# Sixteen half products ahead of the scan's first chunk in place of thirteen, and one function table loaded ahead of softplus

## The chip, the cores and the metric

The kernel runs on one core of one Trainium2 chip. The metric is the time of the program on the device in microseconds (us), the median of several runs; lower is better. The core has five engines that run at the same time and wait for each other by semaphores: TensorE (PE, matrix products; its weight loads are told apart as PEld), VectorE (DVE), ScalarE (ACT, activation functions and copies), GpSimd (POOL) and SyncE (SP, which issues most of the transfers between DRAM and the on-chip memory).

## The reference, cut to what matters

A network of four layers works on an image x of 1024 channels by 64 x 64 pixels in fp32. Each layer adds its output to x, and takes x normalized over groups of 32 channels.

- Layer 0 is a scan over the channels, layers 1 and 3 are pointwise products with a 1024 x 1024 matrix and a bias.
- Layer 2 is a selective scan. Its input is multiplied by a 3072 x 1024 matrix and passed through silu, which gives three parts of 1024 channels: `x_ssm`, `res` and `gate`. `x_ssm` goes through a convolution of width 3 along the pixels and silu, and from it 34 numbers per pixel are made: for each of two heads a step `dt = softplus(...)`, eight values B and eight values C. For each head the pixels are put in an order of its own, and a state of 512 x 8 numbers runs over the 4096 pixels: `h = exp(dt * A) * h + dt * B * x`, `y = C . h + D * x`. Then `y` goes back into image order, and the layer's output is `silu(W_out (y * silu(gate) + res))`.

Softplus is computed as `max(v, 0) + log(1 + exp(-|v|))`, with a correction of the rounding.

## The kernel before, in words

**The products.** A product with a 1024 x 1024 matrix is done by Strassen's scheme (in Winograd's form) on halves: 7 products of half matrices in place of 8. The pixels are in 8 blocks of 512, taken as 4 pairs; a pair gives the two columns of the scheme. `run` goes over the pairs, and `multiply` goes for each pair over two groups `g` of output channels, with 7 products each in the order `b21, b11, b22, t2, t3, t1, t4`. Each product takes one tile of weights (`weights`, L827, issued by SP, five tiles in turn) and one set of right sides (`B`), and adds into two PSUM banks, one for each of two blocks `o` of 128 output channels. `multiply` hands over control after the first block and after the second. What lies between two such points is a *half product*, or unit: 4 matrix products of 128 x 128 by 128 x 512. In the profile each fp32 product is two records of line L844, so a unit is 8 records. When a product is complete, its results are taken: `put` makes a copy (ScalarE), `add` adds to it (VectorE).

**Layer 2 in stages.** First the matrix of `x_ssm` (`WX`) is run over all pairs, with the convolution (L1068, L1071), the turn into pixel rows (L1090, L1092) and the 34 numbers following behind. `finish(pair)` takes the 34 numbers of a pair of blocks, makes softplus of `dt` and writes rows into a table `tok_d` in DRAM, one for each head and pixel. Its steps on ScalarE are Abs (L1194), Exp (L1195) and Ln (L1205), and between and around them stand VectorE's splits of numbers into a coarse and a fine part (L1188, L1190), the steps of the correction (L1200 to L1208) and the transfers to `tok_d` (L1225, L1227), by SP and for the last pair's second head by GpSimd. `finish` runs for each of the four pairs; the first three lie within the products of `WX`, and the last one stands between the last units there and the scan.

Then comes the scan, 74 chunks of 56 pixels of each head. For chunk k, GpSimd gathers its rows from `tok_d` by an indirect transfer (L1321), all of the last `finish` being in the table first; ScalarE makes `ds` (L1329), TensorE makes sums and turns (`turn_rows`, L1335 and L1336), VectorE spreads the decays (`spread_decay`, L1342 to L1350), ScalarE takes Exp (L1418), TensorE crosses B with C (`cross`, L1357), VectorE weighs (`weigh`, L1365 to L1370, into `G`), TensorE applies (`apply`, L1374, `py`), ScalarE hands 8 rows of state for each head to the next chunk (L1377) and copies the result (L1379), and GpSimd scatters it to DRAM (L1383). The steps of the loop are pipelined: step k turns chunk k+1, weighs and applies chunk k-1 and crosses chunk k.

**What fills the scan.** The matrix of `res` (`WR`) doesn't depend on the scan. Its 112 units are handed out by `next_units(upto)`, one at a call as long as fewer than `upto` are given. Eight are given while the last convolutions run, the others up to `first` ahead of chunk 0, and the rest are spread evenly over the loop's 76 steps, at most two in a step:

```python
total, first, given = NP * 2 * NG * 7, 13, 0
...
for k in range(5):
    gather(k)
while given < first:
    next_units(total)
    if len(silus) > 3:
        activate(4)
step_sums(0)
for k in range(-1, NK + 1):
    upto = first + (k + 2) * (total - first) // (NK + 2)
```

For `WR`, `put` is `put2b` (L1030, a ScalarE copy into a tile `rg`), `add` is `add2b` (L1034, a VectorE add), and of finished tiles four at a time are passed through silu by `activate` (L1040) and stored by SP (L1042). During the scan GpSimd also makes sums of weights for layer 3 (`sum_weights2`, L468 to L500, `s` in the profile).

After the scan layer 2's gate and output products and layer 3 follow as one long stage in two levels of the scheme (`two_steps`, L1727).

**The order of the work.** The engines PE, DVE, ACT and POOL are in `tc.manual_schedule` throughout layer 2, so that they take instructions about in the order in which the program writes them; SP is not. ScalarE holds one set of function tables at a time; where the next function needs another set, an instruction ACT_TABLE_LOAD stands ahead of it, put there by the compiler. `nc.scalar.preload_act_table_set(name)` writes such a load into the program by hand, with the set of that name.

Of the kernel before, what the change touches and what calls it, by code (L numbers as in the profile page):

```python
# [50 lines left out]
NG = KH // OG  # L51
NP = NB // 2
# [42 lines left out]
def tile_net(ctx: ExitStack, tc: tile.TileContext, x, par_d, cst_d, w_d, w2_d, dbcw_d, out):  # L95
    nc = tc.nc
# [4 lines left out]
    def ps_tp(name):  # L101
        return psum.tile([P, FB], F32, tag="tp", name=name)
# [798 lines left out]
    def run(pairs, mats, make, put, add, before=None, after=None, last_eng=None, fine=False, tell=False, B=None, begun=None, quick=False):  # L901

        def sets(i):
            B = begun if begun and i == 0 else {"name": f"{mats[0]}_{pairs[i]}"}

            def steps():
                if before is not None:  # L910
                    before(pairs[i])
                yield from b_sets(B, lambda t, ct, col: make(t, ct, 2 * pairs[i] + col), quick=quick or i == 0,
                                  eng=last_eng if i == len(pairs) - 1 else None)
            return B, steps()


        if B is None:
            B, steps = sets(0)
            for _ in range(5 if begun is None else 0):
                next(steps)  # L920
        else:
            steps = iter(())
        for i, pair in enumerate(pairs):
            late = steps
            nxt, steps = sets(i + 1) if i + 1 < len(pairs) else (None, iter(()))
            left = 7 * NG * len(mats)
            for m in mats:
                for half in multiply(m, B, lambda o, c, ps: put(m, o, 2 * pair + c, ps),
                                     lambda o, c, ps: add(m, o, 2 * pair + c, ps), fine, begun and i == 0):
                    if half:  # L930
                        yield True
                        if half == "rest":
                            for _ in range(5):
                                next(late)
                        continue
                    if tell:
                        yield False
                    left -= 1
                    next(steps if left < 5 else late, None)
                    yield  # L940
            if after is not None:
                after(pair)
            last_B[0], B = B, nxt

    def normed(norm):
        def make(t, ct, nb):
            scale, bias = norm[ct]
            nc.scalar.activation(t, X[nb][:, ct, :], AF.Identity, bias=bias, scale=scale)  # L948
        return make
# [95 lines left out]
    with tc.tile_pool(name="l2a", bufs=2) as pa, tc.tile_pool(name="l2a2", bufs=1) as pa2, \  # L1045
# [11 lines left out]
        def tok_rows(t0, q, n, c0, h):  # L1057
            return tok_d[h * N + t0 : h * N + t0 + q * P, c0 : c0 + n].rearrange("(q p) c -> p q c", p=P)
# [91 lines left out]
        def finish(pair):  # L1150
            n = 2 * TPB
            yield
            acc = accs[pair].rearrange("p b (h f) -> p b h f", h=HEADS)
            if pair == NP - 1:

                nc.vector.memset(acc[:, n], 0.0)
                nc.scalar.activation(end, end, AF.Silu)
                pe = ps_tp("end_pt")
                nc.tensor.transpose(pe[:CT, :P], end, ident)
                et = pa.tile([CT, P], F32, name="end_t", bufs=1)  # L1160
                nc.scalar.copy(et, pe[:CT, :P])
                for h in range(HEADS):
                    nc.sync.dma_start(tok_d[h * N + N - 1 : h * N + N, :DH].rearrange("a (b c) -> (a b) c", c=P),
                                      et[h * KH : (h + 1) * KH, :])
                pz = ps_tp("end_dbc")
                for o in range(CT):
                    nc.tensor.matmul(pz[:1, : HEADS * NF], end[:, o : o + 1], both[:, o, P:], start=(o == 0), stop=(o == CT - 1))
                nc.vector.tensor_tensor(accs[pair][:1, n], pz[:1, : HEADS * NF], dbcb[:1], ALU.add)
                n += 1


            def t(name):
                w = pa.tile([P, 2 * TPB + 1, HEADS], F32, tag=f"sp_{name}", name=f"sp_{name}{pair}", bufs=1)
                return w[:, :n]

            f = acc[:, :n]
            v, m, e, u, d = t("v"), t("m"), t("e"), t("u"), t("d")
            lots = [(0, TPB, row), (TPB, TPB, row)]
            if pair == NP - 1:
                lots = [(0, TPB, row), (TPB, 3, spare[0]), (TPB + 3, n - TPB - 3, spare[1])]  # L1180

            def split(b0, q, to, at, c):
                for h in range(HEADS):
                    x = f[:, b0 : b0 + q, h, c : c + S].unsqueeze(2).to_broadcast([P, q, 2, S])
                    parts = to[:, :q, h, at : at + KW].rearrange(
                        "p b (a c) -> p b a c", c=HS)[:, :, :, h * S : (h + 1) * S]
                    hi, lo = parts[:, :, HI[at]], parts[:, :, LO[at]]
                    nc.vector.tensor_scalar(hi.bitcast(I32), x.bitcast(I32), 12, 12, ALU.logical_shift_right,  # L1188
                                            ALU.logical_shift_left)
                    nc.vector.tensor_tensor(lo, x, hi, ALU.subtract)  # L1190

            nc.vector.tensor_copy(v, f[:, :, :, 0])
            nc.vector.tensor_scalar(m, v, 0.0, None, ALU.max)
            nc.scalar.activation(e, v, AF.Abs)  # L1194
            nc.scalar.activation(e, e, AF.Exp, scale=-1.0)  # L1195
            for i, lot in enumerate(lots):
                if i == 0 or lot[2] is not row:
                    split(*lot, CF, 1 + S)

            nc.vector.tensor_scalar(u, e, 1.0, None, ALU.add)  # L1200
            nc.vector.tensor_scalar(d, u, -1.0, None, ALU.add)
            nc.vector.tensor_tensor(d, e, d, ALU.subtract)
            nc.vector.reciprocal(v, u)
            nc.vector.tensor_tensor(d, d, v, ALU.mult)
            nc.scalar.activation(u, u, AF.Ln)  # L1205
            nc.vector.tensor_tensor(u, u, d, ALU.add)
            nc.vector.tensor_tensor(u, u, m, ALU.add)
            nc.vector.tensor_tensor(f[:, :, :, 1 : 1 + S], f[:, :, :, 1 : 1 + S],  # L1208
                                    u.unsqueeze(3).to_broadcast([P, n, HEADS, S]), ALU.mult)
            for i, (b0, q, to) in enumerate(lots):  # L1210
                if i and to is row:
                    yield
                    yield
                    split(b0, q, to, CF, 1 + S)
                split(b0, q, to, BF, 1)
                nc.vector.tensor_copy(to[:, :q, :, DT], u[:, b0 : b0 + q])
                t0 = pair * 2 * FB + b0 * P - 1
                full = min(q, 2 * TPB - b0)
                for h in range(HEADS):
                    dma = nc.gpsimd if h and pair == NP - 1 else nc.sync  # L1220
                    if t0 < 0:
                        dma.dma_start(tok_d[h * N : h * N + P - 1, DH:], to[1:, 0, h, :])
                        dma.dma_start(tok_rows(t0 + P, q - 1, NF2, DH, h), to[:, 1:q, h, :])
                    else:
                        dma.dma_start(tok_rows(t0, full, NF2, DH, h), to[:, :full, h, :])  # L1225
                    if full < q:
                        dma.dma_start(tok_d[h * N + N - 1 : h * N + N, DH:], to[:1, full, h, :])  # L1227

        forget(LATE)
        with tc.manual_schedule(engines={E_.DVE, E_.PE, E_.Pool, E_.Activation}):  # L1230
# [5 lines left out]
            for half in run(EARLY + LATE, [WX], normed(norm2), put2a, add2a, before2,  # L1236
# [26 lines left out]
                if i > 14 and i % 14 == 4:  # L1263
                    ends = finish(i // 14 - 1)
# [15 lines left out]

            forget(EARLY)
            units = run([3, 2] + EARLY, [WR], normed(norm2), put2b, add2b, before2, fine=True, B=last_B[0])
            total, first, given = NP * 2 * NG * 7, 13, 0

            def next_units(upto):
                nonlocal given
# [16 lines left out]
            for _ in finish(NP - 1):  # L1303
                pass
# [548 lines left out]
```

## Time and profile before

| what | us |
|---|---|
| median of 3 runs | 2696.77 (2696.16 to 2699.23) |
| the profiled execution, whole | 2699.02 |
| its span, first to last instruction | 2696.9 |
| TensorE busy | 2568.1 (95%) |
| VectorE busy | 1833.7 (68%) |
| ScalarE busy | 1084.6 (40%) |
| GpSimd busy | 1217.9 (45%) |
| matrix products of layers 1 and 2 up to the scan's end (L844) | 1200.6 |
| the scan, from chunk 0's first matrix product to the last unit | about 1149 to 1627 |

The profiled execution is 2.1 us longer than its span (what lies around it) and 2.25 us longer than the median. Times in the profile's views are counted from the start of the span. Busy times are totals over the whole; an engine that is 95% busy may still stand still where a stage begins, so the stage around the change has to be read by its own times. A matrix product's duration as listed overlaps the next one's: a record of L844 lasts 0.60 us but the next one starts 0.43 us later. In a timeline the number in brackets is the time that the engine stood idle ahead of the instruction, and behind the arrow stands what ended it.

### The profile page before, as it was taken

To read this page: it belongs to the slowest core of one execution; us is meant where nothing else is said; L and a number is where in the kernel's file an instruction comes from. 1 tells how busy PE (TensorE), PEld (TensorE's weight loads), DVE (VectorE), ACT (ScalarE), POOL (GpSimd) and SP (SyncE) were. 2 spreads that over 40 slices of the span, in tenths; PEclk is the share of its full clock that TensorE was granted. 3 is DMA by queue.
4 is the path that set the end of the run, shared out by engine and by line. 5 is a ranking of instruction groups with operands and counts; after the bars stand their busy time and mean duration, and the time that the engine had idled before them with its cause. 6 is when DMAs were issued, how large, how long until landed. Compare 5 with 4: busy or idle time off the path is not lost.

```text
span 2696.9 us, 30618 instructions
## 1 busy us (share of the span) xinstructions
PE 2568.1 (95%) x9520; PEld 1714.4 (64%) x9520; DVE 1833.7 (68%) x3870; ACT 1084.6 (40%) x1839; POOL 1217.9 (45%) x1100
## 2 busy tenths in 40 slices
PE   4788999999999999999999999999999999899998
PEld 3674444444555555444444447888888888788887
DVE  7996866655555654367787775577585676877877
ACT  3783110103656554465767664332243233311220
POOL 4154123232133243136474635575575565554544
PEclk9898999999999999999999999999999999999999
DMA  7245467547555577477667846889899798788896
GB/s 290 102 165 203 147 226 257 182 135 242 152 168 134 145 192 192 119 233 237 212 209 232 303 155 193 236 242 296 223 300 268 240 312 226 257 301 294 302 323 212
DMA packets 422741, 597.22 MB, mean 221 GB/s; under 512 B 141972, under 2 KB 210707, under 8 KB 419508
## 3 DMA queue, kind: packets, MB, share of 16 engines
q1 hardware_dynamic: 298020, 367.89, 42.7%
q10 hardware_dynamic: 91456, 136.33, 14.4%
q0 software_dynamic: 33104, 91.04, 13.3%
q8 instruction: 77, 1.26, 0.2%
q14 instruction: 84, 0.69, 0.1%
HBM read 435.10 MB, written 160.05 MB: 221 GB/s over the span
## 4 chain that ended last, share of the span: by engine, by line
PE 79%; DVE 10%; ACT 7%; DMA 2%; issue 1%; SPq 0%; POOL 0%; DVEq 0%; ACTq 0%; POOLq 0%
PE mm L844 36%; PE q_P6P L1727 5%; PE q_P5P L1727 5%; PE q_P7P L1727 5%; PE q_P2P L1727 5%; PE q_P4P L1727 5%; PE q_P3P L1727 5%; PE q_P1P L1727 5%; PE l2pt L1090 2%; PE py L1374 2%; DVE xt L632 1%; DVE cvp L1071 1%; DVE stats L554 1%; ACT b L948 1%; ACT xt L598 1%
## 5 line engine op out<-in xcount | busy, mean ns | idle before, releaser
L844 PE MATMUL mm<-t,w 128*128 128x512 f32 x1536 | 686.1, 598 | 0.0
L844 PE MATMUL mm<-b,w 128*128 128x512 f32 x1152 | 514.5, 598 | 4.0 <-ACT b L948 2.9
L844 PEld LDWEIGHTS mm<-t,w 128*128 128x128 f32 x1536 | 287.5, 191 | 323.6 <-issue 318.2
L844 PEld LDWEIGHTS mm<-b,w 128*128 128x128 f32 x1152 | 216.1, 191 | 252.6 <-issue 240.9
L1383 POOL DMA_INDIRECT y_rows<-g,dst x74 | 73.8, 997 | 198.2 <-ACT g L1379 166.6
L1071 DVE SCALAR_TENSOR_TENSOR cvp<-xs,par,cvp 128x512 f32<-128x512 f32 x128 | 95.4, 754 | 76.9 <-ACT cvp L1068 74.6
L1696 ACT COPY qQ<-q_P5P 128x512 f32<-128x512 f32 x48 | 28.1, 586 | 294.1 <-PE q_P5P L1727 278.3
L468 POOL TENSOR_TENSOR s<-s 128x256 f32<-128x256 f32 (+3 forms) x120 | 130.6, 1093 | 7.5
L1377 ACT COPY g<-py 8x512 f32<-8x512 f32 x146 | 83.9, 574 | 107.9 <-PE py L1374 106.9
L1122 DVE TENSOR_TENSOR xs<-mm,xs 128x512 f32<-128x512 f32 x64 | 41.8, 685 | 118.1 <-PE mm L844 118.1
L1098 POOL TENSOR_TENSOR acc<-l2xt,acc 128x136 f32<-128x136 f32 x56 | 29.2, 522 | 191.9 <-ACT l2xt L1092 191.0
L963 DVE SCALAR_TENSOR_TENSOR image<-mm,par,image 128x512 f32<-128x512 f32 x64 | 47.2, 747 | 95.3 <-PE mm L844 95.3
L1090 PEld LDWEIGHTS l2pt<-both,cv 128*128 128x128 f32 x512 | 76.2, 190 | 36.3 <-issue 22.5
L802 POOL TENSOR_TENSOR t<-t,b 128x512 f32<-128x512 f32 x40 | 55.7, 1420 | 93.8 <-DVE t L802 93.7
L948 ACT ACTIVATE b<-image,gnl_bias,gnl_r_r 128x512 f32<-128x512 f32 x48 | 36.9, 807 | 143.3 <-PE mm L844 130.6
L1495 ACT ACTIVATE qb<-x_x_b,gn_bias,gn_r_r 128x512 f32<-128x512 f32 x64 | 48.8, 807 | 112.2 <-DVE qQ L1657 36.0
L1727 PE MATMUL q_P4P<-t_t,wq_P4P 128*128 128x256 f32 x384 | 92.5, 384 | 1.4 <-DVE qV L1704 1.4
L1727 PE MATMUL q_P1P<-t_b,wq_P1P 128*128 128x256 f32 x384 | 91.7, 383 | 1.5 <-POOL t_b L1491 1.5
L1704 DVE TENSOR_TENSOR qV<-q_P4P,qV 128x512 f32<-128x512 f32 x96 | 64.9, 687 | 38.6 <-PE q_P4P L1727 37.0
L1491 POOL TENSOR_TENSOR t_t<-qt 128x512 f32<-128x512 f32 x23 | 29.6, 1288 | 136.3 <-DVE qt L1491 76.5
L1727 PE MATMUL q_P5P<-t_t,wq_P5P 128*128 128x256 f32 x384 | 90.8, 379 | 0.0
L1727 PE MATMUL q_P6P<-t_t,wq_P6P 128*128 128x256 f32 x384 | 90.7, 379 | 0.0
(419 smaller groups left out, 6004.7 us busy)
## 6 DMA issues: line engine op xcount, KB each, us to landing
w<-s_d SPq DMA_DIRECT2D x96, 512.0 KB, 4.8
w<-in_w_dram SPq DMA_DIRECT2D x72, 512.0 KB, 4.3
x_x_b<-x_d ACTq DMA_DIRECT2D x28, 1024.0 KB, 6.1
image<-x_d SPq DMA_DIRECT2D x12, 2048.0 KB, 10.9
wq_P6P<-s_d SPq DMA_DIRECT2D x84, 256.0 KB, 5.0
wq_P7P<-s_d SPq DMA_DIRECT2D x84, 256.0 KB, 6.1
wq_P5P<-s_d SPq DMA_DIRECT2D x84, 256.0 KB, 3.6
wq_P3P<-s_d SPq DMA_DIRECT2D x84, 256.0 KB, 3.7
```

Of the source, the lines that this page charges most:

```text
L468: eng.tensor_tensor(out, a, b, ALU.subtract)
L802: eng.tensor_tensor(B[name][k], B[one][k], B[two][k], ALU.subtract)
L844: nc.tensor.matmul(to[o], w[:, k, o * P : (o + 1) * P], B[name][k], start=(fresh and k == 0), stop=(k == KH - 1), skip_group_check=True)
L948: nc.scalar.activation(t, X[nb][:, ct, :], AF.Identity, bias=bias, scale=scale)
L1071: nc.vector.scalar_tensor_tensor(cv, xo[:, at + t : at + t + FB], pcol("dww", 3 * o + t), cv, ALU.mult, ALU.add)
L1090: nc.tensor.matmul(pt[:, q * NV : (q + 1) * NV], cv[:, (q0 + q) * P : (q0 + q + 1) * P], both[:, o, :], start=True, stop=True)
L1374: nc.tensor.matmul(py, G2[k % 2], rows[k][:, :DH], start=True, stop=True)
L1377: nc.scalar.copy(rows[k + 1][h * LC : h * LC + S, :DH], py[h * LC : h * LC + S])
L1383: nc.gpsimd.indirect_dma_start(out=y_views[k % len(y_views)][:, :], out_offset=bass.IndirectOffsetOnAxis(ap=dst_[:, k : k + 1], axis=0), i ...
L1495: nc.scalar.activation(tile_of(j, name)[:, k], held[j, "x", name][:, k], AF.Identity, bias=bias, scale=scale)
L1704: nc.vector.tensor_tensor(to, ps, to, ALU.add)
L1727: nc.tensor.matmul(ps[:, o, :], w[:, k, o * P : (o + 1) * P], rhs[:, k, :], start=(new and o == 0 and k == 0), stop=(k == 1), skip_group_c ...
```

## The change

Two lines. In `finish`, ahead of Abs, a load of the table set `natural_log_exp_and_others` is written into the program; it is not limited to the last pair, so it stands there four times. And 16 units in place of 13 are given ahead of the scan's chunk 0, so that 96 in place of 99 are spread over its 76 steps. The three are the second half of `t4` of the first group, and both halves of `b21` of the second group.

```diff
@@ -1191,6 +1191,7 @@
             nc.vector.tensor_copy(v, f[:, :, :, 0])
             nc.vector.tensor_scalar(m, v, 0.0, None, ALU.max)
+            nc.scalar.preload_act_table_set("natural_log_exp_and_others")
             nc.scalar.activation(e, v, AF.Abs)
             nc.scalar.activation(e, e, AF.Exp, scale=-1.0)
             for i, lot in enumerate(lots):
@@ -1280,7 +1281,7 @@
             forget(EARLY)
             units = run([3, 2] + EARLY, [WR], normed(norm2), put2b, add2b, before2, fine=True, B=last_B[0])
-            total, first, given = NP * 2 * NG * 7, 13, 0
+            total, first, given = NP * 2 * NG * 7, 16, 0
```

## The prediction

> **What bounds the kernel now.** I read the slices first (TensorE at 9 tenths nearly everywhere), then the chain of waits (79% TensorE), then the timelines of TensorE, ScalarE and VectorE where the scan begins. TensorE's timeline there, columns start, length, engine, line, work, and in brackets the idle time before it:
>
> ```profile
> 1124.63 14.86 PE L844 MATMUL mm<-t,w 128*128 128x512 f32 x34
> 1148.86 0.98 PE L1335 MATMUL pr<-cst,g 128*128 128x192 f32 x2 [9.38 <-ACT ds L1329]
> 1149.63 0.53 PE L1336 MATMUL pr<-ds,cst 128*128 128x64 f32 x2
> 1149.95 5.68 PE L844 MATMUL mm<-t,w 128*128 128x512 f32 x8
> 1155.48 0.49 PE L1335 MATMUL pr<-cst,g 128*128 128x192 f32 x2
> 1155.80 0.33 PE L1336 MATMUL pr<-ds,cst 128*128 128x64 f32 x2
> ```
>
> The reader sees the end of the 13 half products that `first` puts ahead of the scan (each is 8 records of L844), then 9.38 us of nothing, then chunk 0. The half product after the hole takes 5.68 us; later ones take 3.65. The stretches (length, busy of TensorE, weight loads, VectorE, ScalarE, GpSimd, granted clock, DMA share, GB/s) show why, and how full the scan is after it:
>
> ```profile
> 1139.00:1150.00 11.00, 1.62 (x7) 1.17 (x5) 0.00 (x0) 0.35 (x1) 7.86 (x13) 0.72 0.79 229
> 1150.00:1156.00 6.00, 6.00 (x14) 2.84 (x13) 3.08 (x8) 2.50 (x4) 0.52 (x1) 0.66 0.79 314
> 1160.00:1628.00 468.00, 456.91 (x1285) 227.53 (x1283) 356.47 (x796) 316.72 (x551) 244.82 (x242) 1.00 0.70 224
> ```
>
> The clock falls to about 0.7 through the hole and returns by 1156. From 1160 to 1628 us TensorE idles 11.1 us in 468: the scan's length is TensorE's work, 99 half products and the 74 chunks' own matmuls.
>
> What the hole waits for is a chain: softplus of the last pair, the split rows, their transfers to `tok_d` (landing 1139.7), gather 0 (issued 1141.88), `ds` of chunk 0 at 1148.51. Its first part, on ScalarE and then VectorE:
>
> ```profile
> 1125.65 0.22 ACT L1194 ACTIVATE sp_e<-sp_v 128x18 f32<-128x18 f32 x1 [1.25 <-DVE sp_v L1192]
> 1125.89 1.28 ACT L1195 ACT_TABLE_LOAD   x1
> 1127.18 0.22 ACT L1195 ACTIVATE sp_e<-sp_e 128x18 f32<-128x18 f32 x1
> 1127.31 0.57 ACT L1030 COPY rg<-mm 128x512 f32<-128x512 f32 x1
> 1127.89 1.28 ACT L1205 ACT_TABLE_LOAD   x1
> 1129.19 0.22 ACT L1205 ACTIVATE sp_u<-sp_u 128x18 f32<-128x18 f32 x1
> ```
> ```profile
> 1129.44 0.18 DVE L1206 TENSOR_TENSOR sp_u<-sp_u,sp_d 128x18 f32<-128x18 f32 x1 [0.66 <-ACT sp_u L1205]
> ```
>
> Two loads of 1.28 us, but VectorE, busy with the splits of L1188 and L1190 until 1127.8, loses only the 0.66 us ahead of L1206.
>
> **What the Trainium skill says.** "ScalarE: Activation LUTs", "Table sets: the hidden batching unit": one set, natural_log_exp_and_others, holds both exp and ln, and abs is in every set; so the added load should make those of Exp and Ln unnecessary. The trace agrees in kind: Abs and the copies bring no load here, and Exp and Ln each bring one, from different sets. Its section "What ACT_TABLE_LOAD costs" gives 1283 ns and 1380 ns of drain. The load agrees (1283 ns); the drain doesn't show, Exp follows 0.01 us after its load; I use 1.28. "TensorE: Matmul & The Clock Gate", "What's actually happening", says that the clock is halved after about 3.4 us of idling and needs as long a busy time to come back. The trace agrees: 9.38 us idle, then some 6 us at 0.66.
>
> **The change, part by part.**
>
> *Three half products moved.* 24 records of L844 that ran in the scan run ahead of chunk 0. In the chain of waits 8 records take 3.44 us, so 3 take 10.3 us. TensorE finished unit 13 at 1139.36 (34 records of 0.43 us from 1124.74); unit 16 should end at 1149.7, so the hole is filled and overrun by 0.8 us. Can they run there? Unit 14 is the rest of `t4`, 15 and 16 are `b21` of the second group. Their right sides are the B tiles just used. Loads run five products ahead on SP: the three weights from the input tensor at 1103.0, 1109.9 and 1120.7 are in order `t4`, `b21` and `b11`, ahead of the row transfers. Their PSUM bank is the one that `t1` leaves, and VectorE's last L1034 on it starts by 1138. So nothing should stop them.
>
> What else moves with them: two VectorE adds of `t4` (L1034, 0.68 us each) at about 1143, when VectorE is empty; and two ScalarE copies of `b21` (L1030, 0.59 us each), the second after unit 16's end. On ScalarE `ds` of chunk 0 may stand behind this copy. Then it runs at 1150.2 to 1150.6 and the second matmul pair of chunk 0 (L1336) waits for it; if it goes ahead, there is no wait. I price it 0 to 0.6 us. Their `rg` tiles come from memory of the earlier pools, free at 1139.7 when the row transfers land. On SP the weights of a later product, held at 1155.67 until unit 14 was done, go out near 1145, between the gathers: 0.5 MB at the 0.4 MB per us that the DMA slices show there at most is 1.3 us (estimate). Gather 0, at 1148.5 now, would come by 1149.1 at worst with the 0.66 us from below, and TensorE is busy until 1149.7. On GpSimd nothing moves.
>
> *The clock.* With no hole, chunk 0's four records take 0.50 us, in place of 1.29, and the unit after them 3.49, in place of 5.48 (all by the chain of waits): 2.8 us.
>
> Sum at the start of chunk 1's matmuls (1155.6 before): chunk 0 starts 0.8 us later (1149.7 for 1148.9), 2.8 us come back, 0 to 0.6 go to `ds`: 1.4 to 2.0 us earlier. From there the scan has 3 half products fewer: 10.3 us. Together 11.7 to 12.3.
>
> *Given back.* The scan has 76 steps; 23 hold two half products now, 20 after. A step of one half product takes 5.07 us. In the one at 1601 VectorE ends G at 1603.8 and `py` uses it at 1605.24: 1.4 us of slack. Where VectorE or ScalarE has a burst in such a step TensorE waits, as these rows (total, times, longest) of the waits from 1160 to 1628 us say:
>
> ```profile
> PE py L1374 <- DVE G L1370: 4.7, 4, 1.4
> PE pr L1336 <- ACT ds L1329: 3.5, 4, 0.9
> PE py L1374 <- ACT rg L1040: 1.5, 1, 1.5
> ```
>
> 9.7 us in 9 places. Three more short steps, and another alignment of all, may remove some or add some: I take 0.7 us more, with -3 and +6 as bounds.
>
> *The function table.* It is in `finish` for all four pairs: 4 loads in, 8 out, 5.1 us less of ScalarE. In the last pair it can run from 1124.4, when ScalarE is idle for 1.25 us, and end about when `sp_v` is there. Exp comes 1.2 us earlier but VectorE is not waiting for it; Ln comes earlier and saves the 0.66 us. In the new order gather 0 is no longer what TensorE waits for, so this is worth 0 on the path; it covers the DMA delay above. In the other three pairs TensorE is busy throughout but for 1.79 us at 909.6, where VectorE's sort is late; there VectorE may gain up to 0.55 us. I take 0.3, with 0 to 0.6. If the load, which depends on no data, slips ahead of a Silu, that pair pays two loads more, 2.6 us of ScalarE, still largely covered.
>
> **Sum:** 12.0 + 0.3 - 0.7 = 11.6; I take **11.3 us**, the low side of the `ds` wait. The profiled execution took 2699.02 us (span 2696.9), so it would give 2687.7; against the median of the runs, 2696.77, it is 2685.5.
>
> **Rivals.**
> - *Half of it given back* (the short steps become bound by the chain weigh, G, `py`). For it: only 1.4 us of slack. Against it: most short steps show no wait. Five more waits of 1.2 us: gain 5 to 7, 2690.5.
> - *No change.* Units 14 to 16 don't run in the hole (a bank, a weight, an order on an engine), or the scan is paced by its recurrence, so that its start sets its end. Against it: 97.6% busy, and weights there by 1121. Time 2695 to 2697.
> - *Slower.* The place is the one-unit step. If the shift of three units puts the bursts of VectorE (two adds 1.28 and a difference L802 1.20 in a row) into steps without a second unit all along, each costs up to 1.5 us. It decides when waits rise by more than 12 us, from 11 to 23; slower by over 0.2% takes 28 us, 19 steps at 1.5 us, in place of 9. Then 2703. Against it: the number of bursts per unit is fixed and the spread of steps nearly the same.
> - *It doesn't do what it says:* the preload leaves a load at Exp or Ln. Then the last part costs 0.66 us of the cover and no more than 1 us.
>
> **How the numbers follow.** 0.2% is 5.4 us, about what a measurement can tell from no change: faster means below 2691.4. Full gain 0.74, half 0.15 (two thirds of it below that line), no change 0.06, slower 0.05. So faster 0.84, same 0.11, slower 0.05. The range from 2682.0 takes 3 us of waits removed and some spread of runs; to 2692.0 it takes the case of half.
>
> **What would show it.** Right: no idle at TensorE between 1124 and 1149, the first L1335 near 1149.7 and within 0.6 us its L1336, then 3.5 us units at clock 1.00; 41 table loads in place of 45, none at Exp and Ln of `finish`; the last L844 near 1616. Wrong: a bracket of some us ahead of a unit or of the first L1336, or waits of `py` for G or for ScalarE above 15 us in the scan. The whole falls if the scan's end stays near 1627.

## The result, and the profile after

| | before | after |
|---|---|---|
| median of 6 runs each, us | 2697.82 (2695.36 to 2700.26) | 2684.88 (2680.42 to 2686.91) |
| ratio of the run times, 95% interval | | 0.9948 (0.9938 to 0.9959) |
| the profiled execution, whole, us | 2699.02 | 2685.99 |
| its span, us | 2696.9 | 2684.1 |
| table loads on ScalarE | 45 | 41 |

The kernel became faster by 12.9 us in the medians, or by 14.0 us by the ratio (0.52%; 11.1 to 16.7 by its interval). The profiles of both kernels are single executions. TensorE's timeline of the changed kernel at the start of the scan (start, length, engine, line, work, idle time ahead of it):

```profile
1124.54 18.29 PE L844 MATMUL mm<-t,w 128*128 128x512 f32 x42
1142.67 7.03 PE L844 MATMUL mm<-b,w 128*128 128x512 f32 x16
1149.54 0.49 PE L1336 MATMUL pr<-cst,g 128*128 128x192 f32 x2
1150.62 0.43 PE L1337 MATMUL pr<-ds,cst 128*128 128x64 f32 x2 [0.60 <-ACT ds L1330]
1150.89 3.65 PE L844 MATMUL mm<-b,w 128*128 128x512 f32 x8
```

Lines below `finish` are one higher than before, so L1336 is `pr` of chunk 0. There is no hole: 42 and 16 records of L844 run through to 1149.5. Chunk 0 waits 0.60 us for `ds`, and the unit after it takes 3.65 us in place of 5.68. The clock and the busy share of the same stretches as before (length, then busy time of TensorE, weight loads, VectorE, ScalarE, GpSimd, then clock, DMA share, GB/s):

```profile
1139.00:1150.00 11.00, 11.00 (x27) 4.75 (x26) 1.38 (x2) 0.85 (x2) 8.38 (x13) 1.00 0.85 261
1150.00:1156.00 6.00, 5.40 (x18) 2.97 (x18) 2.94 (x10) 2.96 (x6) 0.00 (x0) 1.00 1.02 403
```

The clock stays at 1.00. ScalarE around softplus of the last pair and around `ds` of chunk 0 (cut at the dots), and VectorE's step that waited for Ln:

```profile
1124.33 1.28 ACT L1194 ACT_TABLE_LOAD   x1
1125.63 0.22 ACT L1195 ACTIVATE sp_e<-sp_v 128x18 f32<-128x18 f32 x1
1125.75 0.57 ACT L1030 COPY rg<-mm 128x512 f32<-128x512 f32 x1
1126.22 0.22 ACT L1196 ACTIVATE sp_e<-sp_e 128x18 f32<-128x18 f32 x1
1128.52 0.22 ACT L1206 ACTIVATE sp_u<-sp_u 128x18 f32<-128x18 f32 x1 [2.08 <-DVE sp_v L1204]
...
1149.74 0.59 ACT L1030 COPY rg<-mm 128x512 f32<-128x512 f32 x1 [2.73 <-PE mm L844]
1150.22 0.58 ACT L1330 ACTIVATE ds<-cst,g 128x64 f32<-128x64 f32 x2
```
```profile
1128.80 0.18 DVE L1207 TENSOR_TENSOR sp_u<-sp_u,sp_d 128x18 f32<-128x18 f32 x1
```

One load ahead of Abs, none at Exp or Ln. Ln now waits 2.08 us for VectorE, and L1207 has no bracket: counted from the first unit after `end_dbc`, it comes 0.56 us earlier than in the kernel before (4.26 us for 4.82), while 0.66 was forecast. Below the dots `ds` stands behind the copy of `b21`. The waits of TensorE in the scan (total, times, longest), from 1160 to 1613 us:

```profile
PE py L1375 <- DVE G L1371: 3.5, 5, 1.4
PE pr L1337 <- ACT ds L1330: 1.7, 2, 0.9
PE py L1375 <- ACT rg L1040: 1.5, 1, 1.5
PE py L1375 <- ACT g L1380: 0.5, 2, 0.3
```

Together 7.2 us. In the kernel before, the same stretch has the three rows that the prediction shows and 0.4 us of the last one, together 10.1.

**One stretch for all comparisons.** What lies ahead of the last `end_dbc` (L1167) and behind the scan differs by up to some microseconds from one execution to another: the first unit after `end_dbc` starts at 1120.9 to 1129.3 us in the fourteen profiles used here, and the part behind the scan takes 1067.6 to 1071.4 us, with no relation to the edits. The stretch between, from this unit to the end of the scan's last unit, repeats better: 488.41 and 488.49 us in two kernels that differ only in the table load. Where TensorE has a hole, it repeats less well (490.15 and 488.82 us in two executions of one program, 502.62 and 502.14 in two kernels with 13 units), for a reason that "A short hole twice" shows. In the kernel before it is 502.62 us, in the changed one 488.41: **14.21 us less**. The whole span lost 12.8, since the part behind the scan took 1.5 us more in this execution (1071.15 for 1069.65).

### The profile page after: what moved, and what is told of

The parts are those of the page before. It is cut to its first block, busy times and chain, and to the rows that moved or that the text cites. A ratio compares the mean times of both kernels' runs of the same rounds, so it can differ in the third digit from the quotient of the medians.

```text
span 2684.1 us, 30608 instructions
## 1 busy us (share of the span) xinstructions
PE 2564.7 (96%) x9520; PEld 1712.4 (64%) x9520; DVE 1833.2 (68%) x3870; ACT 1079.5 (40%) x1835; POOL 1215.3 (45%) x1100
## 4 chain that ended last, share of the span: by engine, by line
PE 80%; DVE 10%; ACT 6%; DMA 2%; issue 1%; POOL 0%; DVEq 0%; ACTq 0%; SPq 0%; POOLq 0%
PE mm L844 36%; PE q_P5P L1728 5%; PE q_P6P L1728 5%; PE q_P7P L1728 5%; PE q_P3P L1728 5%; PE q_P4P L1728 5%; PE q_P2P L1728 5%; PE q_P1P L1728 5%; PE py L1375 2%; PE l2pt L1090 2%; DVE xt L632 1%; DVE cvp L1071 1%; DVE stats L554 1%; ACT b L948 1%; ACT xt L598 1%
## 5 line engine op out<-in xcount | busy, mean ns | idle before, releaser
L844 PE MATMUL mm<-t,w 128*128 128x512 f32 x1536 | 683.9, 596 | 0.0
L844 PE MATMUL mm<-b,w 128*128 128x512 f32 x1152 | 514.4, 598 | 4.0 <-ACT b L948 2.9
L844 PEld LDWEIGHTS mm<-t,w 128*128 128x128 f32 x1536 | 286.9, 191 | 323.1 <-issue 316.3
L844 PEld LDWEIGHTS mm<-b,w 128*128 128x128 f32 x1152 | 216.0, 191 | 252.3 <-issue 241.3
L948 ACT ACTIVATE b<-image,gnl_bias,gnl_r_r 128x512 f32<-128x512 f32 x48 | 37.2, 808 | 141.6 <-PE mm L844 113.3
L1728 PE MATMUL q_P7P<-t_t,wq_P7P 128*128 128x256 f32 x384 | 90.7, 379 | 0.0
L1728 PE MATMUL q_P2P<-t_b,wq_P2P 128*128 128x256 f32 x384 | 90.7, 379 | 0.0
```

The costliest lines, as they stand in the source:

```text
L844: nc.tensor.matmul(to[o], w[:, k, o * P : (o + 1) * P], B[name][k], start=(fresh and k == 0), stop=(k == KH - 1), skip_group_check=True)
L1728: nc.tensor.matmul(ps[:, o, :], w[:, k, o * P : (o + 1) * P], rhs[:, k, :], start=(new and o == 0 and k == 0), stop=(k == 1), skip_group_c ...
```

## The experiments

Busy and idle are TensorE's, taken from the profiled execution of each kernel over that stretch. "Hole" is the idle time ahead of chunk 0, "`ds`" the wait within chunk 0, "other" the rest of the idle time. Where a run has constants as filler, they count as busy (6.9 us). All runs but "before", units_only and warm_only have the table load. The expectations from first14 to first24 count the stretch to the first matrix product of the next stage, which makes it 0.8 to 0.9 us longer than in the table.

| run | stretch | busy | hole | `ds` | other |
|---|---|---|---|---|---|
| before (13 units) | 502.62 | 482.89 | 9.38 | 0 | 10.35 |
| table_only (13) | 502.14 | 482.48 | 9.34 | 0 | 10.32 |
| warm_only (13) | 499.73 | 487.23 | 2.19 | 0 | 10.31 |
| first14 | 495.02 | 482.16 | 5.88 | 0 | 6.98 |
| first15 | 490.15 | 482.03 | 2.07 | 0 | 6.05 |
| first15_again | 488.82 | 480.33 | 2.44 | 0 | 6.05 |
| units_only (16) | 488.49 | 480.26 | 0 | 0.60 | 7.63 |
| after (16) | 488.41 | 480.23 | 0 | 0.60 | 7.58 |
| ds_first (16) | 487.57 | 479.98 | 0 | 0 | 7.59 |
| ds_first17 | 489.18 | 480.14 | 0 | 0 | 9.04 |
| ds_first18 | 486.34 | 480.02 | 0 | 0 | 6.32 |
| first20 | 494.29 | 481.05 | 0 | 3.41 | 9.83 |
| ds_first20 | 490.62 | 480.77 | 0 | 0 | 9.85 |
| first24 | 492.68 | 481.89 | 0 | 3.45 | 7.34 |

### The units alone

```diff
-            total, first, given = NP * 2 * NG * 7, 13, 0
+            total, first, given = NP * 2 * NG * 7, 16, 0
```

> Sixteen units ahead of chunk 0, without the table load in finish. Theory (the hole at TensorE is filled by units, the table load is worth nothing on the path once it is filled): VectorE keeps its 0.66 us wait ahead of L1206 and gather 0 is issued near 1141.9 as before, but TensorE runs on to 1149.5 without a pause and chunk 0 starts there; 11.5 to 13.5 us below the kernel before, the same as the whole change within 0.7 us. Rival (the two table loads, 2.6 us, lie on the path): 2.6 us less gain than the whole change, some 10 us.

Measured: 2686.44 us, ratio 0.9960 (0.9947 to 0.9974) to the kernel before. By the run times alone (a gain of 10.8 us by the ratio, 7.0 to 14.3 by its interval) the rival, with 2.6 us on the path and some 10 us of gain, could not be told from the theory. The stretch tells them apart: it is 488.49 us, 0.08 from the whole change. VectorE still waits 0.66 us for Ln, and it costs nothing there. The rival falls, and all of the gain in the stretch is the units'.

### The table load alone

```diff
+            nc.scalar.preload_act_table_set("natural_log_exp_and_others")
             nc.scalar.activation(e, v, AF.Abs)
```

> The table load in finish, with thirteen units. Theory: Ln comes 0.65 us earlier and with it the row transfers, gather 0 and chunk 0, so the hole at TensorE is 8.7 in place of 9.4 us, and the three earlier pairs give up to 0.6 us: 0.6 to 1.2 us below the kernel before, hardly to be told from it by time. Rival (both loads on the path): hole 6.8 us, 2.6 us below. Rival (the load slips ahead of a Silu): more than 45 table loads, up to 1 us slower.

Measured: 2698.78 us, ratio 1.0001 (0.9992 to 1.0009). The hole is 9.34 us, not 8.7: the expectation missed. Counted from the stretch's start, VectorE's step came 0.56 us earlier, but GpSimd's first memory fill (L1314), which waits for the row transfers, only by 0.3 us (15.2 for 15.5), the issue of gather 0 by 0.3 (16.95 for 17.25), and `ds` of chunk 0 by 0.04 (23.84 for 23.88). So the lead was lost between the row transfers and `ds`; where exactly was not traced. The stretch's 0.48 us less is nearly all in TensorE's busy time (482.48 for 482.89), and it is the clock's and not the load's: the clock came back 4.2 us after chunk 0's start here and 5.2 us after it in the kernel before, so that the unit after the hole took 5.22 us in place of 5.68. With the hole open, too, the load is worth nothing on this path that shows.

Ahead of the stretch it is worth something. TensorE's wait for the sort near 910 us, in the kernel before and in the changed one:

```profile
911.43 0.66 PE L370 MATMUL sort<-cst,turned 128*64 128x128 f32 x2 [1.79 <-DVE swap L358]
911.05 0.66 PE L370 MATMUL sort<-cst,turned 128*64 128x128 f32 x2 [1.47 <-DVE swap L358]
```

The three kernels without the load wait 1.78 or 1.79 us there, the eleven with it 1.46 or 1.47. That is 0.3 us of TensorE's waiting, too little to show in the run times.

### The clock alone

```diff
+            idle = ps_tp("idle")
+            for i in range(8):
+                nc.tensor.matmul(idle, ident, cst[:, :FB], start=True, stop=True)
             step_sums(0)
```

This is the kernel before, with 13 units; the products' result is not used.

> The kernel before with 8 matrix products of constants (two units' worth, 6.9 us, their result unused) in the hole ahead of chunk 0. Tells what the clock alone is worth. Theory (the clock drops for the idling and costs 2.8 us): hole 9.4 becomes 2.5 us at most of idling, chunk 0 starts at the same 1148.9, its four records take 0.5 in place of 1.3 us and the unit after it 3.5 in place of 5.5 us: 2.8 us below the kernel before. Rival (the slow records are not due to idling but to chunk 0's operands or to the DMA traffic there): no difference.

Measured: 2696.33 us, ratio 0.9990 (0.9982 to 0.9999), 2.7 us by the ratio. TensorE's timeline:

```profile
1139.85 7.03 PE L1403 MATMUL idle<-cst 128*128 128x512 f32 x16
1149.07 0.56 PE L1335 MATMUL pr<-cst,g 128*128 128x192 f32 x2 [2.19 <-DMA res_d<-rg]
1149.47 0.33 PE L1336 MATMUL pr<-ds,cst 128*128 128x64 f32 x2
1149.63 3.65 PE L844 MATMUL mm<-t,w 128*128 128x512 f32 x8
```

Chunk 0 starts no later than before (23.92 us from the stretch's start, 24.23 before), with useless work ahead of it, and the unit after it takes 3.65 us. The stretch is 2.89 us shorter, 2.5 of it in the busy time (487.23 less 6.88 of constants is 480.35, for 482.89). The rival, in which chunk 0's operands or the DMA traffic make the records slow, expected no difference and falls. The low clock is the price of idling, and the term of the prediction stands.

### `ds` ahead of the copies

```diff
             while given < first:
+                if given == first - 1:
+                    step_sums(0)
                 next_units(total)
                 if len(silus) > 3:
                     activate(4)
-            step_sums(0)
```

> The changed kernel with step_sums(0), which makes ds of chunk 0, written ahead of the sixteenth unit, so that it stands before the two copies of b21 on ScalarE. Theory (the 0.6 us of TensorE's wait between L1336 and L1337 comes from that order alone): ds runs near 1148, the wait is gone, and the scan ends 0.6 us earlier than in the changed kernel, 12 to 14 us below the kernel before. Rival (gather 0 itself lands at 1150 among the weights): the wait stays at 0.6 us.

Measured: 2682.67 us, ratio 0.9944 (0.9930 to 0.9958). Chunk 0 has no wait, and the stretch is 487.57 us, 0.84 less than with the change. So the 0.6 us was ScalarE's order alone. `ds` starts 23.7 us after the stretch's start (23.9 in the kernel before), so the weights that now go out between the gathers did not delay gather 0 either. This version has a shorter stretch than both kernels; in the run times it can't be told from the change.

### Other numbers of units

```diff
-            total, first, given = NP * 2 * NG * 7, 16, 0
+            total, first, given = NP * 2 * NG * 7, 14, 0    # or 15, 20, 24
```

> The changed kernel with 14 units ahead of chunk 0. Measured is the stretch from the first unit after end_dbc (L1167) to the first matrix product of the next stage (q_P1P): 503.5 us in the kernel before, 489.3 in the changed one. Theory (TensorE's work in this stretch is fixed; it costs what TensorE idles and what the low clock adds): a hole of 5.9 us stays, long enough for the clock to fall, so 3.4 us less than before plus or minus 3 us for other waits in the scan: 500 (497 to 503). Rival (the start of chunk 0 and the scan's own steps set the end): chunk 0 starts as before, 503.5.

> The changed kernel with 15 units ahead of chunk 0, the same stretch. Theory (idling and clock): a hole of 2.4 us stays, as in the run with constants in the hole, so the clock doesn't fall: 6.9 + 2.8 = 9.7 us less than before, 493.8, plus or minus 3 us for other waits. Rival (the low clock comes with any hole): 496.6. Rival (the start of chunk 0 sets the end): 500.7 to 503.5.

> The changed kernel with 20 units ahead of chunk 0: four more than fit, so that chunk 0 starts 13.8 us later than in the changed kernel and the scan has 92 units. Theory (the scan is TensorE's work): the stretch is the changed kernel's 489.3 plus or minus 3 us of other waits. Rival (the scan is paced by its own chain of steps, and a later start is paid in full): 503.

> As the run with 20, with 24 units ahead: chunk 0 starts 27.5 us later than in the changed kernel, and of 76 steps only 12 hold two units. Theory (the scan is TensorE's work): 489.3 plus or minus 4 us of other waits. Rival (short steps have too little slack, each step taken from two units to one adds a wait of about 1 us): 8 more waits, 497. Rival (a later start is paid in full): 516.

Measured: 2689.45 us with 14, 2686.19 with 15 and 2686.79 with 24 (one time each), and 2689.66 with 20, ratio 0.9969 (0.9959 to 0.9979).

With 14 the stretch is 495.02 us, below the range expected: 3.5 less from the hole, 3.4 less from other waits, and 0.7 less busy time. The rivals in which the start of chunk 0 sets the end fall with 14 (503.5 expected) and, the other way, with 24: chunk 0's matmuls start 27.5 us later than in the changed kernel and the stretch is 4.3 us longer, not 27. The other rival for 24, a wait of about 1 us for each step that goes from two units to one, falls too: its other waits are 7.34 us, for 7.58 in the changed kernel. With 15 the stretch lies at the lower edge of the range expected, but not for the reason given: the clock did fall after a hole of 2.07 us, which the theory excluded, and fewer other waits made up for it. With 20 it is 494.29 us, some 3 us above the range of the theory and 8 below the rival; the larger part of what is too much is a wait of 3.41 us in chunk 0. ScalarE's timeline of this kernel shows where from:

```profile
1162.36 0.59 ACT L1030 COPY rg<-mm 128x512 f32<-128x512 f32 x1 [2.85 <-PE mm L844]
1162.84 1.52 ACT L948 ACTIVATE b<-image,gn2a_bias,gn2a_r_r 128x512 f32<-128x512 f32 x2
1164.26 1.51 ACT L948 ACTIVATE b<-image,gn2b_bias,gn2b_r_r 128x512 f32<-128x512 f32 x2
1165.67 0.57 ACT L1330 ACTIVATE ds<-cst,g 128x64 f32<-128x64 f32 x2
```

The twentieth unit ends a product late in its pair, and four normalizations for the next pair's right sides (L948) come with it. They stand ahead of `ds`. With 24 units twelve come ahead of it, four each with the units 20, 22 and 24; the first eight are over when chunk 0 begins, and the last four make the wait of 3.45 us.

### The same, with `ds` ahead

The edit of "`ds` ahead of the copies" with 20 units, and, with `given == 15` in place of `given == first - 1`, with 17 and 18.

> The kernel with 20 units, with step_sums(0) written ahead of the twentieth unit, so that ds of chunk 0 stands before that unit's copies and before the four normalizations (L948) on ScalarE. Same stretch: 494.3 us with 20 units, 488.4 in the changed kernel. Theory (the 3.4 us at chunk 0 with 20 units is ScalarE's order alone, and the rest of the gap lies in other waits of the scan): the wait between L1336 and L1337 is gone, 490.5 to 491.2. Rival (the later start of chunk 0 costs by itself): above 493.

> 17 units, with step_sums(0) ahead of the sixteenth. Same stretch, 487.6 us with 16 units and step_sums(0) ahead. Theory (TensorE's work of 480 us plus what the scan's other waits are, 6 to 10 us for each of the numbers tried so far, without a trend): 486 to 491, chunk 0 without a wait. Rival (each further unit ahead shortens or lengthens the scan by its 3.4 us): 484 or 491.

> 18 units, with step_sums(0) ahead of the sixteenth. Theory: as with 17, 486 to 491, the difference to 17 only from which of the scan's waits occur. Rival (a trend with the number of units): 481 or 494.

Measured: 490.62, 489.18 and 486.34 us of stretch (2690.98, 2682.64 and 2685.33 us, one time each). With 20 the wait is gone and with it 3.67 us, as the theory has it. With 17 and 18 the stretch lies in the range expected and off both values of the rival with a trend. What is left between the numbers of units is the column "other": 10.35 with 13, 6.98, 6.05, 7.6, 9.04, 6.32, 9.85 with 20 and 7.34 with 24. There is no trend. The waits end on VectorE's `G` and on ScalarE's `ds`, `rg` and `g`, so it is probably a matter of which steps of the scan meet a burst there; this was not traced step by step. 18 units with `ds` ahead have the shortest stretch of all, but one run doesn't make it faster than the change.

### A short hole twice

> The kernel with 15 units once more. With a hole of 2.1 us its unit after chunk 0 took 4.9 us in place of 3.5, though the run with constants showed 3.5 us after a hole of 2.2. If the clock falls for the length of the hole alone, the two can't both repeat: then this run shows 3.5 us, and the stretch is 488.4. If it falls again (4.9 us, 490.2), something else than the hole's length tells the two apart.

Measured: 2685.16 us, stretch 488.82. The first run's timeline of TensorE, and that of the repetition:

```profile
1148.36 0.70 PE L1336 MATMUL pr<-cst,g 128*128 128x192 f32 x2 [2.07 <-DMA s<-in_w_dram]
1148.86 0.52 PE L1337 MATMUL pr<-ds,cst 128*128 128x64 f32 x2
1149.18 5.09 PE L844 MATMUL mm<-b,w 128*128 128x512 f32 x8
```
```profile
1148.66 0.56 PE L1336 MATMUL pr<-cst,g 128*128 128x192 f32 x2 [2.44 <-DMA s<-in_w_dram]
1149.06 0.33 PE L1337 MATMUL pr<-ds,cst 128*128 128x64 f32 x2
1149.22 3.65 PE L844 MATMUL mm<-b,w 128*128 128x512 f32 x8
```

The same program: after 2.07 us of idling the clock fell, after 2.44 it did not. So the length of the hole alone doesn't decide it. The column of the granted clock in the traces shows what does. In each of the fourteen profiles (16 to 20 entries of the clock in each) it changes only at the edges of intervals of 3.41 us, which run on from one end of the execution to the other whatever the program does. Two neighbouring intervals of the first run, cut 0.01 us inside their edges (length, then busy time of TensorE, weight loads, VectorE, ScalarE, GpSimd, then clock, DMA share, GB/s):

```profile
1145.26:1148.65 3.39, 1.32 (x5) 0.51 (x4) 0.00 (x0) 0.35 (x1) 2.59 (x3) 1.00 0.95 329
1148.67:1152.06 3.39, 3.39 (x8) 1.84 (x7) 2.16 (x6) 0.82 (x2) 1.21 (x2) 0.50 1.03 414
```

And two of the repetition:

```profile
1143.83:1147.22 3.39, 2.39 (x6) 0.76 (x4) 0.00 (x0) 0.00 (x0) 2.48 (x4) 1.00 0.96 279
1147.24:1150.64 3.40, 1.98 (x8) 1.30 (x9) 1.06 (x5) 0.35 (x1) 2.48 (x3) 1.00 1.07 400
```

In the first run the whole hole lies in one interval, TensorE is busy for 1.32 us of it, and the next interval has half the clock. In the repetition the longer hole is shared by two intervals with 2.39 and 1.98 us of work, and the clock stays. The other runs agree. The wait of 3.45 us with 24 units leaves 0.10 us of work in one interval, and the next has half the clock; the wait of 3.41 us with 20 units is shared by two (1.54 and 1.84 us of work), and the clock stays, as it does in warm_only (2.87 and 1.75). Where the limit lies was not measured: elsewhere in the profiles intervals with 42 to 54% of work went either way. The kernel before has three intervals at half the clock, and TensorE works in 5.09 us of them:

```profile
1143.90:1153.95 10.05, 5.09 (x9) 2.92 (x10) 2.76 (x7) 2.85 (x5) 5.10 (x6) 0.50 1.00 340
```

Work at half the clock takes twice as long, so half of these 5.09 us, some 2.5 us, is what the low clock costs (an estimate); the busy time is 2.66 us longer than in the changed kernel.

## Why the prediction was right

It forecast 11.3 us less; the stretch gave 14.2, the medians 12.9. Its steps in turn:

- **The hole is filled and overrun by 0.8 us.** Chunk 0 started 25.00 us after the stretch's start, for 24.23: 0.77 later. No weight, bank or right side held the three units up.
- **The clock, 2.8 us.** 2.66 in the busy time; with constants in the hole, 2.54. The "about 0.7" of the prediction was a mean over its windows: the clock was 1.00 up to 1143.80 us and 0.50 from there to 1154.04. The amount depends on where the intervals of 3.41 us fall; with 13 units and the table load it was 2.25.
- **The wait of `ds`, 0 to 0.6 us.** 0.60, the upper end, which the 11.3 us contain (11.7 + 0.3 - 0.7). The prediction left open which of two ScalarE instructions goes first; in the program `ds` of chunk 0 is written behind the copy, and it ran so.
- **The scan has 10.3 us fewer of work, and it is TensorE's work that sets its length.** That the stretch is busy time plus idle time holds of any engine and shows nothing by itself. What shows it is that the needed work is 480 to 482.9 us in all fourteen profiles and the other waits stay between 6 and 10.4 us, while chunk 0's start moves by 28 us between 13 and 24 units: a later start costs the scan no more than these waits and that of `ds`. The excess of the work over 480 is mostly the low clock. The 1.7 us with 24 units are one interval of 3.41 us at half the clock; the 0.8 us with 20 lie mostly in the records of `pr` (50.4 us for 49.4), and why these are longer was not traced.
- **Given back, 0.7 us, with -3 and +6 as bounds.** This is the term that was mis-sized: the other waits fell from 10.35 to 7.58 us, a gain of 2.77 and within the bounds. The prediction took three more short steps for a slight loss. The other numbers of units show that it is no matter of more or fewer short steps, and that 13 was the worst of the eight numbers tried; that it is a matter of where the bursts fall is argued, not shown. For the same reason the last L844 ended at 1612.95 us and not near 1616.
- **The table load is worth nothing on the path, and 0.3 us in the earlier pairs.** Both single edits confirm the first. The second is seen in TensorE's wait for the sort near 910 us, 1.79 us before and 1.47 after; in the start of the stretch, which moves by 8 us between executions, it can't be told.

The balance over the stretch: hole -9.38, clock -2.66, `ds` +0.60, other waits -2.77, together -14.21, the measured difference. The terms of the forecast that belong to the stretch come to 11.0 us (11.3 less the 0.3 of the earlier pairs). That the median of the changed kernel, 2684.88 us, still lies 0.6 us from the forecast 2685.5 is luck in part: the forecast starts from a median of 2696.77 us, which is 2697.82 with three runs more, and the rest of the program varies by more than what the sum lacks.

The rivals don't hold: the units ran in the hole, the other waits fell in place of rising, and no load is left at Exp or Ln.

The Trainium skill's page "ScalarE: Activation LUTs", section "Table sets: the hidden batching unit", was right for this case: the changed kernel has one load for Exp and Ln together, and in the kernel before Abs had none.

## What to carry to other kernels

Where one engine's work sets the length of a long stage, sum what that engine idles and what a low clock adds, and fill the stage's largest hole with independent work of the same engine, a little more than the hole holds; here the clock stayed up with it (1.00 for 0.50). Before placing the filler, list what each piece brings to the other engines' queues: here two copies, and with four pieces more four normalizations, ended up ahead of the one small instruction that the next chunk waits for. Small waits within the pipelined loop moved by up to 4.3 us from one number of units to another without a trend, so take them into the range, not into the forecast.

## What the hardware showed that was not expected

A pause of 2.07 us was followed by 5.09 us for a unit that takes 3.65 otherwise, in one execution, and a pause of 2.44 us by 3.65 in another of the same program. The Trainium skill, "TensorE: Matmul & The Clock Gate", section "What's actually happening", speaks of windows of about 3.4 us that run freely, and of a low clock after at least one idle window. The windows agree with the traces: the clock changes on a grid of 3.41 us, and how a hole lies on it differs from one execution to the next. That a window has to be idle does not agree: one in which TensorE was busy for 1.32 of 3.39 us was enough. The measurement decides. So in this program the same hole cost 1.7 us of busy time in one execution (482.03 for 480.33) and nothing in the other, and two profiles of one kernel with such a hole can differ by that much.
